# A two-layer "macaron" block with an S4D layer: the second feed-forward's weights and norm parameters are loaded from ACT's DMA queue at set points, and the last scans' temporaries move to another buffer

## The chip, the cores and the metric

The kernel runs on one core of one Trainium2 chip. The core has five engines with a queue each: PE (matrix products), DVE (vector work), ACT (scalar functions and copies), POOL (elementwise work) and SP (here it only issues DMAs). An engine takes its instructions strictly in the order of its queue; engines wait for each other through semaphores. The metric is the device time of one execution in microseconds. Three runs of the kernel before gave 1841.8, 1843.71 and 1846.46; the median is 1843.71.

## The reference

The input x is 8 sequences of 2048 positions with 256 channels.

```python
x = x + 0.5 * ffn(layernorm(x), w1, b1, w2, b2)
x = x + s4d(layernorm(x), log_A_real, A_imag, C_re, C_im, log_dt, D, ln_w, ln_b)
x = x + 0.5 * ffn(layernorm(x), w1, b1, w2, b2)

def ffn(x, w1, b1, w2, b2):
    h = relu(x @ w1 + b1)          # 256 -> 1024
    return h @ w2 + b2             # 1024 -> 256

def s4d(x, ...):                   # a state space model, one filter per channel
    K = s4d_kernel(...)            # 256 channels x 2048 positions, 64 modes each
    y = irfft(rfft(x, 2L) * rfft(K, 2L))[:, :L]     # causal convolution
    r = x + (y + x * D)
    return layernorm(r) * ln_w + ln_b
```

Both feed-forwards use the same weights. The norm's parameters ln_w and ln_b belong to the middle layer; the kernel applies them when it reads that layer's result, at the beginning of the second feed-forward's work on a group.

## The kernel before, in words

**Three stages.** `sublayer(..., "a", ...)` is the first feed-forward, then comes the SSM (the calls of `states` and `outputs`), then `sublayer(..., "b")`. A feed-forward takes the tokens in 64 groups of 256. For each group `pre_a` or `pre_b` normalises and transposes the tokens, `up` multiplies by w1 (bank `ph`), ACT and DVE make the two-part hidden values (buffer `hx`), `down` multiplies by w2 (bank `po`), and `post_a` or `post_b` adds the result. The groups are staggered: `lead` steps of preparation run before the first product.

**The SSM.** The convolution is done in 16 chunks of 128 positions. The 256 channels form 32 batches `bt` of 8 channels (4 pairs), and the batches are put into 12 groups `gr`, listed in `PLAN` with a state buffer (`xsA`, `xsB` or `xsE`) and a part of it. Group 8 is batches 22 to 25, group 9 is batches 26 and 27, group 10 is 28 and 29, group 11 is 30 and 31; group 7 is 20 and 21.
- `states(gr)`: for each batch PE projects the chunks onto the states (bank `pv`, line 972, with the loaded matrices `pt`), ACT copies the result to the state buffer (`keep`, line 955). Then a `scan` runs over the chunks, 14 steps of four instructions each (lines 1008 to 1011): two products with the decay factors into temporaries, and two additions to the next chunk's states. Most pairs are scanned by DVE, some by POOL (`POOL_PAIRS`).
- `outputs(gr)`: for each batch SP loads the matrices `tz` (line 1024) and `ot` (line 1038), ACT copies the channels to `uc` (line 1031), PE sums the part within the chunk (line 1043, `uc` with `tz`) and the part from the states (line 1052, the state buffer with `ot`) in two banks `py`, and ACT writes both back to `u` (line 1058, "the evacuation").

`states` runs ahead of `outputs` by three groups (`AHEAD = 3`): program order is outputs 6, states 9, outputs 7, states 10, outputs 8, states 11, outputs 9, 10, 11.

**Buffers.** Tiles that share a tag share a ring of buffers (`BUFS`): a new tile takes the buffer of the tile that was allocated that many allocations earlier, and its first writer waits for the last reader of the old one. The tag `hx` has 4 buffers: the hidden values of the feed-forwards and the copies `uc` of the SSM. The tags `e` and `te` have one buffer each: the two temporaries of DVE's scan steps, and after the last scan the norm's parameters `lnw_sb` and `lnb_sb`. The large buffers `wA` and `wB` hold the weights of the first feed-forward, then the states A and B, then the weights of the second (`wb1` in `wA`, `wb2` in `wB`), so `wb1` can be written when the last group in A (group 8) has been read, and `wb2` when the last in B (group 10) has.

**Order.** A scheduler orders the instructions of each engine by their readiness; `tc.issue_after` puts an instruction behind another one, and `tc.manual_schedule` keeps the engines that it names in program order. `sublayer` uses the latter for ACT and DVE in its lead if it has a list `first` (the first feed-forward has) or if `MB` is set.

**The reload.** After the last group the kernel writes the DMAs that bring back the split weights from DRAM: eight of 256 KB for w1 and four of 512 KB for w2 on SP's queue (lines 1133 and 1137), and ln_w and ln_b, spread over the partitions, on POOL's queue (line 1143). The second feed-forward's first group needs `lnb_sb` on POOL (line 1152), `lnw_sb` on DVE (`y`), `wb1` in `up` and `wb2` in `down`.

Of the kernel before, what the change touches and what calls it, by code (L numbers as in the profile page):

```python
# [10 lines left out]
F32 = mybir.dt.float32  # L11
F32R = mybir.dt.float32r
# [7 lines left out]
P = 128  # L20
# [23 lines left out]
def macaron_s4d_kernel(  # L44
# [17 lines left out]
    nc = tc.nc  # L62
    V = nc.vector
    A_ = nc.scalar
    G_ = nc.gpsimd

    B, L, H = x.shape
    N = c_re.shape[1]
    W = w1.shape[1]
    NJ = L // P  # L70
# [3 lines left out]
    NDC = H // P  # L74
    NFC = W // P
# [6 lines left out]
    PINW = 1  # L82
    NZ = 1
    PINF = 0
    MB = 0
    PINT = 1
    XY = 4
    NU = NFC // 2
# [16 lines left out]
    wpool = ctx.enter_context(tc.tile_pool(name="wpool", bufs=1))  # L105
# [4 lines left out]
    def bank(tag, name):  # L110
        return ps.tile([P, 512], F32, name=name, tag=tag, bufs=BANKS[tag])

    def slot(tag, shape, name, dtype=F32):
        tag = {"sw": "xn"}.get(tag, tag)
        return work.tile(shape, dtype, name=name, tag=tag, bufs=BUFS[tag])
# [23 lines left out]
    w1_dram = dram.tile([2, P, NDC, W], F32, name="w1_dram")  # L139
    w2_dram = dram.tile([2, P, NFC, H], F32, name="w2_dram")  # L140
# [667 lines left out]
    def sublayer(w1t, w2t, pre, post, lead, tag, first=(), background=(), due=()):  # L808
# [32 lines left out]
        ordered = ExitStack()  # L841
        if first or MB:
            ordered.enter_context(
# [78 lines left out]
    PLAN = [E8, ("A", 0, 8), ("A", 8, 16), B16, E8, A16, B16, E8, A16, ("B", 0, 8), ("B", 8, 16), E8]  # L922
# [2 lines left out]
    assert sum(sizes) == NPAIR  # L925
    starts = [sum(sizes[:i]) for i in range(len(sizes))]
    SPAN = {"A": 16, "B": 16, "E": 8}
    TAGS = ("e", "te")
    POOL_PAIRS = [8, 0, 0, 4, 4, 4, 4, 4, 4, 2, 2, 0]
    LASTX = 11  # L930
    OTS = ("xh", "xh", "pl", "xn"), ("xh", "x", "pl", "x")
    TZS = ("xl", "xl", "pl"), ("xl", "x", "pl")
    BH = 4
    BL = 9
    xbuf = {}
    steps = {}

    BEHIND = [BH] * (len(PLAN) - 1) + [BL]

    def states_of(gr):  # L940
        key, at, end = PLAN[gr]
        if key not in xbuf:
            t = wpool.tile([P, 2, SPAN[key], NJ * B], F32, name=f"xs{key}", tag=f"w{key}")
            G_.memset(t[:, :, :, 0:B], 0.0)
            xbuf[key] = t
        return xbuf[key][:, :, at:end]

    def batches(gr):
        for p0 in range(0, sizes[gr], PB):
            yield p0, (starts[gr] + p0) // PB  # L950
# [6 lines left out]
    def states(gr):  # L957
        xs = states_of(gr)
        for p0, bt in batches(gr):
            pts = []  # L960
            for c in range(2):
                pt = slot("x", [P, PB, P], f"pt{bt}_{c}")
                nc.sync.dma_start(out=pt, in_=pt_dram[bt].rearrange("k (c l m) -> k c l m", c=2, m=P)[:, c])
                pts.append(pt)
            pv = [
                bank(tag, f"pv{bt}_{ri}").rearrange("p (l m) -> p l m", l=PB)
                for ri, tag in enumerate(("oo", "tb")[bt % 2])
            ]
            for l in range(PB):
                for ri in range(2):  # L970
                    for c in range(2):
                        nc.tensor.matmul(
                            pv[ri][c * N : (c + 1) * N, l, :], pts[c][:, l, ri * N : (ri + 1) * N],
                            u[:, :, BCH * bt + 2 * l + c, :],
                            start=True, stop=True, skip_group_check=True,
                        )
            keep(xs, [v[:, :, 0:CB] for v in pv], slice(p0, p0 + PB), slice(B, NJ * B))
        on_dve = sizes[gr] - POOL_PAIRS[gr]
        if on_dve:
            for _ in scan(gr, V, 0, on_dve, 1, NJ - 1, TAGS):  # L980
                pass
        if POOL_PAIRS[gr]:
            for _ in scan(gr, G_, on_dve, sizes[gr], 1, NJ - 1, ("g", "gt")):
                pass
# [4 lines left out]
    def scan(gr, E, p0, p1, j0, j1, tags):  # L989

        n = p1 - p0
        shape = [P, 2, n, B]
        xv = states_of(gr)[:, :, p0:p1].rearrange("p r g (j b) -> p r g j b", b=B)
        gs = slice(starts[gr] + p0, starts[gr] + p1)
        wr_b = wr_c[:, gs].unsqueeze(1).unsqueeze(3).to_broadcast(shape)
        wi_b = wi_c[:, :, gs].unsqueeze(3).to_broadcast(shape)
        for j in range(j0, j1):
            t1, t2 = (
                slot(tag, [P, 2, 8 if tag in ("g", "gt") else 16, B], f"{tag}_{gr}_{j}")[:, :, 0:n]
                for tag in tags  # L1000
            )
            with ExitStack() as behind:
                if E is V and prev(gr) in steps:

                    before = steps[prev(gr)]
                    at = min(BEHIND[gr] + j - j0, len(before) - 1)
                    behind.enter_context(tc.issue_after(before[at].ins))
                E.tensor_mul(t1, xv[:, :, :, j, :], wr_b)  # L1008
                E.tensor_mul(t2, xv[:, ::-1, :, j, :], wi_b)  # L1009
                E.tensor_add(xv[:, :, :, j + 1, :], xv[:, :, :, j + 1, :], t1)  # L1010
                ins = E.tensor_add(xv[:, :, :, j + 1, :], xv[:, :, :, j + 1, :], t2)  # L1011
            if E is V:
                steps.setdefault(gr, []).append(ins)
            yield

    def outputs(gr):
        xs = states_of(gr)
        for p0, bt in batches(gr):
            py, tzs, ucs, ots = [], [], [], []
            for c in range(2):  # L1020
                tz = slot(TZS[gr >= LASTX][(2 * bt + c) % 3], [P, PB, P], f"tz{bt}_{c}")

                row = kpad[BCH * bt + c, 1:]
                nc.sync.dma_start(
                    out=tz,
                    in_=bass.AP(row.tensor, row.offset, [[1, P], [2 * KROW, PB], [1, P]]),
                )
                tzs.append(tz)

                uc = slot("hx", [P, PB, P], f"uc{bt}_{c}")  # L1030
                A_.copy(
                    uc.rearrange("p l (q m) -> p l q m", q=NQ),
                    u[:, :, BCH * bt + c : BCH * (bt + 1) : 2, :].rearrange("p q l m -> p l q m"),
                )
                ucs.append(uc)
            for ri in range(2):
                ot = slot(OTS[gr >= LASTX][(2 * bt + ri) % 4], [P, PB, P], f"ot{bt}_{ri}")
                nc.sync.dma_start(out=ot, in_=o_dram[bt][:, ri * PB * P : (ri + 1) * PB * P])
                ots.append(ot)
            for c in range(2):  # L1040
                py.append(bank("h", f"py{bt}_{c}").rearrange("p (l m) -> p l m", l=PB))
                for l in range(PB):
                    nc.tensor.matmul(
                        py[c][:, l, :], ucs[c][:, l, :], tzs[c][:, l, :],
                        start=(l == 0), stop=False, skip_group_check=True,
                    )

            for l in range(PB):
                for ri in range(2):
                    for c in range(2):  # L1050
                        cs = slice(c * N, (c + 1) * N)
                        nc.tensor.matmul(
                            py[c][:, l, :], xs[cs, ri, p0 + l, :], ots[ri][cs, l, :],
                            start=False, stop=(l == PB - 1 and ri == 1), skip_group_check=True,
                        )
            for c in range(2):

                A_.copy(
                    uo[:, :, bt, :, c::2], py[c].rearrange("p l (q m) -> p q m l", q=NQ)
                )  # L1060

    def some(j0, j1):

# [53 lines left out]
        {"half": NG // 2, "tables": NG * 3 // 4},  # L1117
    )

    for gr in (1, 2, 3):  # L1120
        states(gr)
    for gr in range(len(sizes)):
        outputs(gr)
        if gr and gr + AHEAD < len(sizes):
            states(gr + AHEAD)


    wb1 = wpool.tile([P, 2, NDC, W], F32R, name="wb1", tag="wA")
    wb2 = wpool.tile([P, 2, NFC, H], F32R, name="wb2", tag="wB")
    for f in range(0, W, W // 4):  # L1130
        fs = slice(f, f + W // 4)
        for i in range(2):
            nc.sync.dma_start(out=wb1[:, i, :, fs].bitcast(F32), in_=w1_dram[i][:, :, fs])
    for f in range(0, NFC, 4):
        fs = slice(f, f + 4)
        for i in range(2):
            nc.sync.dma_start(out=wb2[:, i, fs].bitcast(F32), in_=w2_dram[i][:, fs])


    lnw_sb = slot("e", [P, H], "lnw_sb")  # L1140
    lnb_sb = slot("te", [P, H], "lnb_sb")
    for dst, src in ((lnw_sb, ln_w), (lnb_sb, ln_b)):
        nc.gpsimd.dma_start(out=dst, in_=src.partition_broadcast(P))

    def pre_b(g):
        by_dma = g >= DMA_B
# [70 lines left out]
```

## Time and profile before

| what | value |
|---|---|
| three runs | 1841.8, 1843.71, 1846.46 us; median 1843.71 |
| the profiled execution | 1849.43 us; span of its instructions 1847.7 us |
| first feed-forward, to the last down-projection of the chain | 864.7 us |
| SSM, to the last evacuation | 1087.2 us |
| second feed-forward, from its first up-projection | 1097.4 us |
| busy over the span | PE 95%, DVE 86%, ACT 66%, POOL 39% |
| granted TensorE clock, mean | 0.978 |

In rows of the timeline the columns are the start (us from the span's first instruction), the duration of the merged row, the engine, the line, the operation with the tiles that it writes and reads, and the number of merged instructions; what stands in brackets is the idle time before it and what ended it. A row of an `L1043` or `L1052` matmul counts two records for each matmul of the program, so 16 `uc` records and 32 `ot` records are one batch. "SPq" is a DMA issued by SP's queue.

### The profile page before, as it was taken

The numbers are of one execution on the slowest core, as the hardware profiler recorded it, in microseconds if no ns is written. First come the engines' busy times: TensorE is split into PE (matmuls) and PEld (weight loads), VectorE is DVE, ScalarE is ACT, GpSimd is POOL, SyncE is SP. The second block draws the span as 40 slices with busy tenths as digits, with TensorE's granted clock in tenths as the row PEclk, the third lists the DMA queues.
The fourth block names the chain that finished last, engine by engine and source line by source line (L and its number), as shares of the span: only waits on it lengthen the run. The fifth ranks groups of instructions, "written<-read, shape, count | busy, mean of one in ns | idle before, by whom it ended". The sixth has DMA issues, their size and how long they took to land.

```text
span 1847.7 us, 43034 instructions
## 1 busy us (share of the span) xinstructions
PE 1757.2 (95%) x15147; PEld 1721.2 (93%) x15147; DVE 1593.6 (86%) x5027; ACT 1212.3 (66%) x2931; POOL 717.0 (39%) x963
## 2 busy tenths in 40 slices
PE   7999799998899999999999879999999999999998
PEld 7999789898888999998888879999999999999998
DVE  5899997998899977775999958989899999999995
ACT  6776556766676776765555436777777777776675
POOL 1016761888478413211588612222222222222220
PEclk9999899999999999999999979999999999999999
DMA  5112233887787943334788833333333333333331
GB/s 186 41 50 58 59 101 90 229 240 236 213 242 228 265 115 102 98 97 127 241 244 250 261 115 87 92 92 92 93 92 92 92 92 92 92 92 91 91 92 51
DMA packets 299451, 245.44 MB, mean 133 GB/s; under 512 B 169954, under 2 KB 242402, under 8 KB 298722
## 3 DMA queue, kind: packets, MB, share of 16 engines
q1 hardware_dynamic: 297456, 241.75, 44.8%
q8 instruction: 119, 1.95, 0.4%
q0 software_dynamic: 800, 0.67, 0.3%
q14 instruction: 98, 0.80, 0.1%
q10 hardware_dynamic: 978, 0.26, 0.1%
HBM read 91.89 MB, written 111.15 MB: 110 GB/s over the span
## 4 chain that ended last, share of the span: by engine, by line
PE 51%; DVE 9%; issue 3%; DMA 2%; POOL 2%; ACT 1%; SPq 0%; POOLq 0%; DVEq 0%; ACTq 0%
PE ph_b L789 19%; PE po_b L799 19%; PE po_a L799 6%; PE ph_a L789 6%; DVE e L1008 2%; DVE te L1009 2%; DVE xsA L1011 1%; DVE xsA L1010 1%; DVE xsB L1010 1%; DVE xsB L1011 1%; DMA wb<-w_dram 1%; DVE xsE L1011 1%; DMA pt_b<-xp 0%; DVE xsE L1010 0%; POOL xsB L1011 0%
## 5 line engine op out<-in xcount | busy, mean ns | idle before, releaser
L799 PE MATMUL po_a<-wa,hx_a 128*128 128x256 f32 x3072 | 462.1, 288 | 11.1 <-DVE hx_a L859 10.4
L789 PE MATMUL ph_a<-xh_a,wa 128*128 128x256 f32 x2048 | 461.6, 289 | 5.7 <-ACT xh_a L736 3.0
L789 PE MATMUL ph_b<-xh_b,wb 128*128 128x256 f32 x2048 | 443.4, 284 | 1.1 <-ACT xh_b L736 0.7
L799 PE MATMUL po_b<-wb,hx_b 128*128 128x256 f32 x3072 | 443.2, 284 | 0.0
L799 PEld LDWEIGHTS po_a<-wa,hx_a 128*128 128x128 f32 x3072 | 410.0, 195 | 17.6 <-DVE hx_a L859 16.2
L799 PEld LDWEIGHTS po_b<-wb,hx_b 128*128 128x128 f32 x3072 | 400.0, 192 | 0.9
L789 PEld LDWEIGHTS ph_a<-xh_a,wa 128*128 128x128 f32 x2048 | 362.8, 197 | 8.0 <-ACT xh_a L736 3.6
L857 ACT ACTIVATE ph_a<-ph_a,b_sb 128x256 f32<-128x256 f32 x512 | 228.8, 449 | 200.5 <-PE ph_a L789 190.0
L789 PEld LDWEIGHTS ph_b<-xh_b,wb 128*128 128x128 f32 x2048 | 352.9, 193 | 2.1 <-ACT xh_b L736 1.2
L857 ACT ACTIVATE ph_b<-ph_b,b_sb 128x256 f32<-128x256 f32 x512 | 229.8, 449 | 168.3 <-PE ph_b L789 162.3
L789 PE MATMUL ph_a<-xl_a,wa 128*128 128x256 f32 x1024 | 294.7, 290 | 20.9 <-DVE xl_a L770 11.3
L1152 POOL TENSOR_TENSOR xb<-xb,lnb_sb 128x512 f32<-128x512 f32 x64 | 92.4, 1446 | 514.3 <-DMA xb<-x_dram 232.4
L789 PE MATMUL ph_b<-xl_b,wb 128*128 128x256 f32 x1024 | 287.2, 285 | 0.7 <-DVE xl_b L770 0.2
L859 DVE TENSOR_TENSOR hx_a<-ph_a,hx_a 128x256 fp32r<-128x256 f32 x512 | 207.5, 412 | 77.8 <-ACT hx_a L858 76.1
L859 DVE TENSOR_TENSOR hx_b<-ph_b,hx_b 128x256 fp32r<-128x256 f32 x512 | 205.0, 410 | 33.2 <-ACT hx_b L858 31.3
L789 PEld LDWEIGHTS ph_a<-xl_a,wa 128*128 128x128 f32 x1024 | 201.6, 197 | 23.2 <-DVE xl_a L770 12.3
L720 POOL TENSOR_TENSOR xa<-xa,hb 128x512 f32<-128x512 f32 x64 | 84.3, 1317 | 354.9 <-DVE xn_a L694 243.1
L789 PEld LDWEIGHTS ph_b<-xl_b,wb 128*128 128x128 f32 x1024 | 197.5, 193 | 1.9 <-DVE xl_b L770 1.4
L858 ACT CAST hx_a<-ph_a 128x256 fp32r<-128x256 f32 x512 | 188.4, 374 | 13.2 <-PE po_a L799 1.6
L858 ACT CAST hx_b<-ph_b 128x256 fp32r<-128x256 f32 x512 | 187.7, 374 | 11.3
L720 POOL TENSOR_TENSOR xb<-xb,hb 128x512 f32<-128x512 f32 x64 | 87.9, 1373 | 52.4 <-DVE t_r L681 26.3
L118 DVE SCALAR_TENSOR_TENSOR y<-u,mv_r,lnw_sb 128x256 f32<-128x256 f32 x128 | 82.8, 688 | 4.8 <-PE pt_b L727 0.9
(257 smaller groups left out, 2824.9 us busy)
## 6 DMA issues: line engine op xcount, KB each, us to landing
xa<-in_L_attn_x_dram SPq DMA_DIRECT2D x64, 256.0 KB, 2.8
x_dram<-xa SPq DMA_DIRECT2D x64, 256.0 KB, 2.3
o<-u SPq DMA_DIRECT2D x32, 512.0 KB, 4.0
pv<-planes SPq DMA_DIRECT2D x32, 512.0 KB, 3.6
pt<-u SPq DMA_DIRECT2D x32, 512.0 KB, 3.4
ot<-o SPq DMA_DIRECT2D x64, 256.0 KB, 3.7
tz<-kpad SPq DMA_DIRECT2D x64, 256.0 KB, 4.2
xb<-x_dram SPq DMA_DIRECT2D x64, 256.0 KB, 2.7
```

Of the source, the lines that this page charges most:

```text
L118: return V.scalar_tensor_tensor(out=o, in0=a, scalar=s, in1=b, op0=op0, op1=op1)
L720: G_.tensor_add(xt, xt, hb2.unsqueeze(1).to_broadcast([P, NTB, H]))
L789: nc.tensor.matmul(ph, wt[wp][:, dc, fs], xp[:, dc, :], start=(n == 0), stop=(n == 3 * NDC - 1))
L799: nc.tensor.matmul(po[:, i, :], hp[:, tsl], wt[wp][:, fc, :], start=(fc == 0 and i == 0 and n == 0), stop=(fc == NFC - 1 and n == 2), skip ...
L857: A_.activation(ph, ph, AF.Relu, bias=b1_sb[:, fc : fc + 1])
L858: last[A_] = A_.copy(hh, ph)
L859: last[V] = V.tensor_sub(hl, ph, hh.bitcast(F32))
L1008: E.tensor_mul(t1, xv[:, :, :, j, :], wr_b)
L1009: E.tensor_mul(t2, xv[:, ::-1, :, j, :], wi_b)
L1010: E.tensor_add(xv[:, :, :, j + 1, :], xv[:, :, :, j + 1, :], t1)
L1011: ins = E.tensor_add(xv[:, :, :, j + 1, :], xv[:, :, :, j + 1, :], t2)
L1152: G_.tensor_add(xt, xt, lnb_sb.unsqueeze(1).to_broadcast([P, NTB, H]))
```

## The change

The temporaries of DVE's scans from group 9 on (`LASTE = 9`) no longer live in `e` and `te`: both halves of one `hx` tile are used. This leaves `e` and `te` free after group 8, and `lnw_sb` and `lnb_sb` are allocated there. A generator, `late_loads`, issues the loads from ACT's queue in three parts: ln_w and ln_b, then w1 in two DMAs of 1 MB, then w2 in two of 1 MB. Each part is put behind the last evacuation of the first batch of a group: groups 9, 10 and 11. The DMAs on SP's and POOL's queues are gone. `MB = 1` keeps ACT and DVE in program order in the lead of the second feed-forward.

```diff
-    MB = 0
+    MB = 1
...
-    TAGS = ("e", "te")
     POOL_PAIRS = [8, 0, 0, 4, 4, 4, 4, 4, 4, 2, 2, 0]
     LASTX = 11
+    LASTE = 9
...
+    evacs = {}
...
-            for _ in scan(gr, V, 0, on_dve, 1, NJ - 1, TAGS):
+            for _ in scan(gr, V, 0, on_dve, 1, NJ - 1, ("hx",) if gr >= LASTE else ("e", "te")):
...
+            if tags == ("hx",):
+                both = slot("hx", [P, 2, 2, 16, B], f"hx_{gr}_{j}")
+                t1, t2 = (both[:, i, :, 0:n] for i in range(2))
+            else:
+                t1, t2 = (
+                    slot(tag, [P, 2, 8 if tag in ("g", "gt") else 16, B], f"{tag}_{gr}_{j}")[:, :, 0:n]
+                    for tag in tags
+                )
...
-                A_.copy(
+                done = A_.copy(
                     uo[:, :, bt, :, c::2], py[c].rearrange("p l (q m) -> p q m l", q=NQ)
                 )
+            evacs.setdefault(gr, []).append(done)
...
+    def late_loads():
+        for dst, src in ((lnw_sb, ln_w), (lnb_sb, ln_b)):
+            nc.scalar.dma_start(out=dst, in_=src.partition_broadcast(P))
+        yield
+        for i in range(2):
+            nc.scalar.dma_start(out=wb1[:, i].bitcast(F32), in_=w1_dram[i])
+        yield
+        for i in range(2):
+            nc.scalar.dma_start(out=wb2[:, i].bitcast(F32), in_=w2_dram[i])
+        yield
+
+    LOADS = {LASTE: 1, LASTE + 1: 1, len(PLAN) - 1: 1}
     for gr in (1, 2, 3):
         states(gr)
     for gr in range(len(sizes)):
         outputs(gr)
         if gr and gr + AHEAD < len(sizes):
             states(gr + AHEAD)
-    wb1 = wpool.tile([P, 2, NDC, W], F32R, name="wb1", tag="wA")
-    wb2 = wpool.tile([P, 2, NFC, H], F32R, name="wb2", tag="wB")
-    for f in range(0, W, W // 4):
-        fs = slice(f, f + W // 4)
-        for i in range(2):
-            nc.sync.dma_start(out=wb1[:, i, :, fs].bitcast(F32), in_=w1_dram[i][:, :, fs])
-    for f in range(0, NFC, 4):
-        fs = slice(f, f + 4)
-        for i in range(2):
-            nc.sync.dma_start(out=wb2[:, i, fs].bitcast(F32), in_=w2_dram[i][:, fs])
-    lnw_sb = slot("e", [P, H], "lnw_sb")
-    lnb_sb = slot("te", [P, H], "lnb_sb")
-    for dst, src in ((lnw_sb, ln_w), (lnb_sb, ln_b)):
-        nc.gpsimd.dma_start(out=dst, in_=src.partition_broadcast(P))
+        if gr == LASTE - 1:
+            lnw_sb = slot("e", [P, H], "lnw_sb")
+            lnb_sb = slot("te", [P, H], "lnb_sb")
+            wb1 = wpool.tile([P, 2, NDC, W], F32R, name="wb1", tag="wA")
+            loads = late_loads()
+        if gr == LASTE + 1:
+            wb2 = wpool.tile([P, 2, NFC, H], F32R, name="wb2", tag="wB")
+        if gr in LOADS:
+            with tc.issue_after(evacs[gr][0].ins):
+                next(loads)
```

More of the change, by code (lines that the diff above doesn't have):

```diff
@@ L997, in scan @@
         for j in range(j0, j1):
[L998 to L1001, printed above, removed]
+            if tags == ("hx",):
[6 more added lines that the diff above has]
+                )
             with ExitStack() as behind:
```

## The prediction

> **What bounds the kernel now.** I read the busy shares, then the chain of waits, then the timeline of each engine from 1005 us to 1100 us, the seam the change touches. The kernel has three stages: the first feed-forward to 864.7 us, the SSM to 1087.15, the second feed-forward from 1097.37. In the second PE is full (499.76 of 500 us from 1300 to 1800) and the order of the first is not touched, so only the seam can move. In the SSM the chain runs along DVE's scans:
>
> ```profile
> 1026.83 0.31 DVE L1008 TENSOR_TENSOR e<-xsB,wr_c 128x96 f32<-128x96 f32 x1
> 1041.62 0.24 DVE L1008 TENSOR_TENSOR e<-xsB,wr_c 128x96 f32<-128x96 f32 x1
> 1055.61 0.28 DVE L1008 TENSOR_TENSOR e<-xsE,wr_c 128x128 f32<-128x128 f32 x1
> 1070.42 0.29 DVE L1011 TENSOR_TENSOR xsE<-xsE,te 128x128 f32<-128x128 f32 x1
> ```
>
> These are the first instructions of scans 9, 10 and 11 and the last of scan 11: back to back, 14 steps each, 1.056, 1.00 and 1.08 us a step. PE works on outputs beside them:
>
> ```profile
> 1024.90 2.05 PE L1043 MATMUL py<-tz,uc 128*128 128x128 f32 x16
> 1042.25 3.71 PE L972 MATMUL pv<-u,pt 128*64 128x128 f32 x64
> 1050.95 2.05 PE L1052 MATMUL py<-ot,xsB 64*128 64x128 f32 x16
> 1057.03 2.05 PE L1043 MATMUL py<-tz,uc 128*128 128x128 f32 x8 [4.03 <-DMA tz<-kpad]
> 1059.00 3.78 PE L1052 MATMUL py<-ot,xsB 64*128 64x128 f32 x16
> 1081.92 2.05 PE L1043 MATMUL py<-tz,uc 128*128 128x128 f32 x16
> 1083.90 2.06 PE L1052 MATMUL py<-ot,xsE 64*128 64x128 f32 x32
> ```
>
> The four batches 22 to 25 (group 8) stand between the first two rows: 4.34 us a batch, while scan 9 runs. So outputs of group g run during scan g+1, and when scan 11 ends (1070.71) little is left: PE is done at 1085.96. It would have been done sooner but for the 4.03 us wait; after it TensorE runs at half clock:
>
> ```profile
> 1050.00:1055.00 5.00, 3.00 (x24) 2.69 (x24) 4.66 (x22) 2.34 (x4) 0.76 (x4) 0.98 1.09 348
> 1055.00:1060.00 5.00, 2.98 (x12) 2.78 (x13) 4.69 (x21) 0.62 (x1) 0.00 (x0) 0.50 0.80 246
> 1070.00:1075.00 5.00, 5.00 (x30) 4.78 (x30) 0.68 (x3) 1.12 (x2) 1.18 (x2) 0.50 0.64 146
> 1075.00:1080.00 5.00, 5.00 (x58) 4.64 (x57) 0.00 (x0) 2.38 (x4) 2.49 (x2) 0.97 0.61 171
> ```
>
> Columns: PE, PEld, DVE, ACT, POOL busy, then granted clock, DMA share and GB/s. The wait comes from SP's queue, where 2 MB of w1 went just ahead of that `tz`:
>
> ```profile
> 1043.05 2.61 SPq L1133 DMA_DIRECT2D wb<-w_dram  x4
> 1046.84 2.77 SPq L1133 DMA_DIRECT2D wb<-w_dram  x4
> 1049.71 0.55 SPq L1024 DMA_DIRECT2D tz<-kpad  x1
> 1078.66 1.75 SPq L1137 DMA_DIRECT2D wb<-w_dram  x4
> ```
>
> Then a front of 10.2 us from the last evacuation to the first up-projection:
>
> ```profile
> 1086.04 1.11 ACT L1058 COPY u<-py 128x512 f32<-128x512 f32 x2 [2.84 <-PE py L1052]
> 1095.47 1.23 PE L727 MATMUL pt_b<-ident,xn_b 128*128 128x128 f32 x4 [9.52 <-DVE xn_b L694]
> 1097.37 1.23 PE L789 MATMUL ph_b<-xh_b,wb 128*128 128x256 f32 x4 [0.68 <-ACT xh_b L736]
> ```
>
> The reloads themselves are not on the path: the last w2 transfer, issued by 1080.4, landed by 1089.97, and its first reader starts at 1102.65. Nor are the norm's parameters: their POOL additions end at 1078.6 while their DVE readers start at 1088.
>
> **The change, part by part.**
>
> *Buffers, the part that decides.* From group 9 on each scan step takes one of the four `hx` buffers for both temporaries; the copies `uc` of every output batch, two each, rotate through the same four. Rotation follows program order: uc of group 6, scan 9, uc of group 7, scan 10, uc of group 8, scan 11, uc of groups 9, 10, 11. In the changed program as built the waits say just that: uc20_0 waits for step 11 of scan 9, uc20_1, uc21_0 and uc21_1 for steps 12 to 14; uc22_0 for step 11 of scan 10; uc26_0 for step 11 of scan 11; in return, scan 10 waits for the `uc` matmuls of batches 20 and 21, scan 11's first step for those of batch 24 (steps 2, 7 and 9 for 24 and 25). Overlap becomes alternation. PE's order moves too: the projections `pv` of groups 10 and 11 (7.4 us) stand ahead of batch 20, their loads ahead of `tz21_1` on SP. Up to `pv27` (1012.4 us) all engines' orders are unchanged.
>
> *Walk to scan 11.* PE ends pv31 near 1023 (7.4 us of work, and loads that take turns in the `x` buffers) and idles until uc20_0: step 11 of scan 9 ends at 1026.83 + 11 x 1.056 = 1038.45, the copy takes 0.62, PE starts at 1039.1. Sixteen idle microseconds put the clock at half, as the 4.03 did. Prices of matmuls: 16 `uc` records 2.0 us at full clock, 4.0 at half (8 took 1.97 from 1057.03 to 1059.00); 32 `ot` records 2.0 when the two halves alternate, but one half alone costs 2.05 for 16 at full and 3.71 at half (rows 1050.95 and 1059.00), and batches 20, 22 and 26 have such stretches. Batch 20: 2.0 + 2.8 + 2.0 + 3.8 = 10.6, to 1049.7; batch 21: `uc` 4.0, then 2.0 with the clock back, to 1055.5. Scan 10 begins on time, since its first step needs only four `uc` matmuls (1041.2 against 1041.62), and loses about 1 us at steps 10 and 12. ACT is in order: uc22_0 stands behind the evacuation of batch 21, so 1057.4. PE: batch 22 with its serial stretches 5.8, batch 23 4.0, first half of batch 24's `uc` 1.0: scan 11 starts at 1068.3, not 1055.61: **+12.7**. If the clock returns within batch 20, batch 21 is out by 1052 and uc22_0 waits for scan 10 alone: 1064.7, **+9.1**. At half clock throughout: 1059.8 + 21.5 = 1081.3, **+25.7**.
>
> *From the end S of scan 11 to the last evacuation.* Before: 1087.15 - 1070.71 = 16.4. After: six batches, 26 to 31, are still to do, where two were. uc26_0 is there at S - 3 x 1.08 + 0.65 = S - 2.6, PE has idled some 5.5 us (half clock again); batch 26 takes 10.6 to S + 8.0, batch 27 6.0 to S + 14.0, four batches at 4.34 to S + 31.4, evacuation 1.2: S + 32.6, **+16.2**. Clock back 4 us sooner: +12.4. Full clock from the start: 5.5 + 5 x 4.05 + 1.2 - 2.6 = S + 24.4, +8.0. Half clock all through (8.0 a batch): about +35.
>
> *Loads on ACT's queue.* Six issues at 0.38 to 0.70 us (the six ACT-queue rows of the first stage), in evacuation gaps of 1.3 us and more: nothing, as `uc` copies run a batch ahead of PE. The second w2 issue waits for the first w1 half; ACT's evacuation of batch 31 stands behind it. w1 is issued after batch 28, some 8.7 us earlier, and the reloads before took 4.2 to 10.0 us to land: 0 to +2, taken +0.5. w1 and w2 have about 20 and 10 us until their readers; w2's margin is the thin one. SP loses 12 issues and POOL two; the 4.03 us wait behind them goes, but lay beside scan 11, and its benefit is inside the tail's count.
>
> The Trainium skill, page "DMA: Bandwidth & Descriptors", section "Rules for kernel authors", speaks against this part: spreading transfers over issuing engines saves issue time only, all share the same 16 DMA engines. The row that bears on it is the DMA share of 1.09 while w1 and `tz` ran together. By the rule w1 would hold up `tz31` by up to those 4.03 us again; without the rule it is 0.
>
> *Program order in the lead of the second feed-forward.* The first group's chain no longer shares DVE with statistics of groups 1 and 2 (the 1.39 us of st_r at 1091.09, 0.35 of mv_r), but y now follows the reciprocals, and the sqrt of group 1 precedes xh on ACT: -1.8 to 0, taken **-1.0**.
>
> **Sum.** Late release 12.7 + 16.2 + 0.5 - 1.0 = +28.4; release within the first batch 9.1 + 12.4 + 0.5 - 1.0 = +21. In the trace the half clock lasted 18 us after 1057.03, where serial `ot` stretches ran, and some 5 us after 868.57 with `pv` matmuls; the new stretches mix both, so I take the middle, +25. The profiled run took 1849.4 (span 1847.7 + 1.7), 5.7 above the median of 1843.7; it would become 1874, the median **1869**. Floor: 9.1 + 8.0 - 1.8 = +15.3, 1859.
>
> The skill's "TensorE: Matmul & The Clock Gate", Part 1, has the clock return after about 3.4 us of sustained work. The 18 us of half clock from 1057 disagree with it. By the rule each restart costs 1.7 us, the first one hidden behind scan 10, and the sum would be about +17, 1861.
>
> **Rivals.** (a) The clock stays low: serial stretches keep it at half through batches 22 to 26. For it: 18 us at 0.50 above. Against: full-array `uc` stretches of 4 us follow, and 1072.86 to 1075.97 brought the clock back. Price +35 to +45: 1879 to 1889. (b) Weights late: if w2's halves, serialized behind w1 and ACT's evacuations, land after the first down-projection, PE waits there; 10.0 us was the longest landing, so +3 to +8 more, 1872 to 1877. (c) Not slower: the shared rotation costs nothing, scans 10 and 11 stay at 1041.62 and 1055.61, groups 9 and 10 are out during scan 11, SP no longer holds `tz27_1`. Then PE ends two batches after 1070.71: 8.1 + 1.2 = 1080.0, -7.1, and -1.0 at the front: 1836. It decides if scan 11 starts before 1060. Against it stand the waits in the built program. (d) The reload is hidden anyway and nothing moves: true of the loads, not of the buffers.
>
> **Numbers.** Likeliest 0.78 (1859 to 1878), (a) 0.12, (b) 0.05, (c) 0.03, (d) 0.02. Range 1857 to 1884. A difference of 0.3% (5.5 us) is what the measurement can tell from none. Slower 0.95, same 0.02, faster 0.03.
>
> **What would show it.** PE idle from about 1023 to 1039 and again around 1077, each followed by a granted clock of 0.5; `uc` copies of ACT released by DVE scan steps; scan 11's start at 1064 to 1070 and end near 1080 to 1085; six output batches behind it; last evacuation near 1112; front of some 9 us. Wrong if scan 11 starts at 1056, if the front shrinks by more than 3, or if PE waits for `wb`.

## The result, and the profile after

| | before | after |
|---|---|---|
| median of five runs each | 1844.91 us (1841.8 to 1848.44) | 1879.24 us (1876.04 to 1880.59) |
| ratio | 1 | 1.0181, 95% interval 1.0164 to 1.0197 |
| profiled execution, its span | 1849.43, 1847.7 us | 1880.59, 1878.8 us |
| first instruction of scan 9 to the end of scan 11 | 43.88 us | 57.92 us |
| end of scan 11 to the last evacuation | 16.44 us | 34.56 us |
| last evacuation to the first up-projection | 10.22 us | 9.45 us |
| the three together, "the seam" | 70.54 us | 101.93 us |

The change makes the kernel slower: 34.3 us by the medians, 31.1 by the two profiled spans. The seam, taken from the first instruction of scan 9 so that the drift of a few microseconds ahead of it drops out, grew by 31.4 (14.0 + 18.1 - 0.8) and so holds all that the two profiles differ by. The 3 us between spans and medians are not explained: the profiled execution before lay 4.5 us above its median, the one after 1.35. Line numbers of the changed kernel are five higher from the scan's lines on.

The timeline of DVE after the change, with the first instructions of scans 9 and 10, the first one of scan 10 that had to wait, then the first and the last instruction of scan 11:

```profile
1025.59 0.31 DVE L1013 TENSOR_TENSOR hx<-xsB,wr_c 128x96 f32<-128x96 f32 x1
1040.48 0.24 DVE L1013 TENSOR_TENSOR hx<-xsB,wr_c 128x96 f32<-128x96 f32 x1
1050.76 0.26 DVE L1013 TENSOR_TENSOR hx<-xsB,wr_c 128x96 f32<-128x96 f32 x1 [0.89 <-PE py L1048]
1068.41 0.29 DVE L1013 TENSOR_TENSOR hx<-xsE,wr_c 128x128 f32<-128x128 f32 x1 [12.84 <-ACT u L1063]
1083.22 0.29 DVE L1016 TENSOR_TENSOR xsE<-xsE,hx 128x128 f32<-128x128 f32 x1
```

Scans 9 and 10 still stand back to back, but scan 11 has 12.84 us of idle DVE ahead of it. (The profile names ACT's evacuation of batch 23, which ends at 1068.36, as its releaser. By the waits of the built program, as the prediction lists them, it waits for `uc` products of batch 24, the first of which end at 1068.30 by PE's timeline; the two lie too close together for the profile to tell them apart.) PE's timeline shows the other half of the alternation:

```profile
1038.02 2.08 PE L1048 MATMUL py<-tz,uc 128*128 128x128 f32 x8 [14.88 <-ACT uc L1036]
1040.03 2.93 PE L1057 MATMUL py<-ot,xsE 64*128 64x128 f32 x12
1048.60 3.78 PE L1048 MATMUL py<-tz,uc 128*128 128x128 f32 x16
1057.27 1.16 PE L1048 MATMUL py<-tz,uc 128*128 128x128 f32 x8 [2.47 <-ACT uc L1036]
1063.18 2.05 PE L1048 MATMUL py<-tz,uc 128*128 128x128 f32 x16
1081.05 2.08 PE L1048 MATMUL py<-tz,uc 128*128 128x128 f32 x8 [5.21 <-ACT uc L1036]
1091.62 3.27 PE L1048 MATMUL py<-tz,uc 128*128 128x128 f32 x16
1108.41 2.06 PE L1057 MATMUL py<-ot,xsE 64*128 64x128 f32 x32 [1.14 <-DMA ot<-o]
1112.85 2.02 PE L1048 MATMUL py<-tz,uc 128*128 128x128 f32 x16 [2.39 <-DMA tz<-kpad]
```

The first, fourth and sixth rows are the starts of batches 20, 22 and 26, each released by a copy `uc`. The copy itself is released by DVE's scan, as ACT's timeline says; the rows after it are the loads on ACT's queue and the last evacuation:

```profile
1037.35 0.62 ACT L1036 COPY uc<-u 128x512 f32<-128x512 f32 x1 [18.71 <-DVE xsB L1016]
1080.38 0.62 ACT L1036 COPY uc<-u 128x512 f32<-128x512 f32 x1 [3.34 <-DVE xsE L1016]
1101.46 0.82 ACTq L1133 DMA_DIRECT2D wb<-w_dram  x2
1110.63 0.81 ACTq L1136 DMA_DIRECT2D wb<-w_dram  x2
1116.95 1.12 ACT L1063 COPY u<-py 128x512 f32<-128x512 f32 x2 [5.31 <-PE py L1057]
```

So DVE's scan waits for the output batches, the output batches wait for the scan, and 14.88 and 5.21 us of PE's time and 12.84 of DVE's are spent waiting. After each long wait the granted clock is low (windows of the changed kernel; columns as in the prediction: PE, PEld, DVE, ACT, POOL busy, granted clock, DMA share, GB/s):

```profile
1045.00:1050.00 5.00, 5.00 (x26) 4.78 (x27) 4.47 (x18) 1.72 (x4) 4.22 (x19) 0.50 0.32 84
1055.00:1060.00 5.00, 2.73 (x22) 2.60 (x22) 0.54 (x3) 4.39 (x9) 0.00 (x0) 1.00 0.46 138
1085.00:1090.00 5.00, 5.00 (x24) 4.55 (x24) 0.00 (x0) 0.62 (x1) 0.00 (x0) 0.50 0.23 61
1100.00:1105.00 5.00, 5.00 (x70) 4.76 (x70) 0.00 (x0) 2.41 (x5) 0.00 (x0) 1.00 0.97 286
```

In the last, full-clock window PE gets through 70 records, in the half-clock ones through 24 to 26; the ratio is more than two because the half-clock windows also hold stretches of `ot` matmuls on one half. After the short wait of 2.47 us (second row) the clock is at 1. The front is the last part:

```profile
1125.52 1.23 PE L727 MATMUL pt_b<-ident,xn_b 128*128 128x128 f32 x4 [8.66 <-DVE xn_b L694]
1127.52 1.23 PE L789 MATMUL ph_b<-xh_b,wb 128*128 128x256 f32 x4 [0.78 <-ACT xh_b L736]
```

No wait for `wb` follows: the weights were there in time.

### The profile page after: what moved, and what is told of

Its sections match the earlier page's. It is cut to its first block, busy times and chain, and to the rows that moved or that the text cites. A ratio compares the mean times of both kernels' runs of the same rounds, so it can differ in the third digit from the quotient of the medians.

```text
span 1878.8 us, 43020 instructions
## 1 busy us (share of the span) xinstructions
PE 1760.8 (94%) x15147; PEld 1725.3 (92%) x15147; DVE 1601.2 (85%) x5027; ACT 1211.5 (64%) x2931; POOL 718.9 (38%) x961
## 4 chain that ended last, share of the span: by engine, by line
PE 56%; DVE 7%; DMA 3%; issue 1%; ACT 1%; DVEq 0%; SPq 0%; ACTq 0%
PE ph_b L789 19%; PE po_b L799 19%; PE po_a L799 6%; PE ph_a L789 6%; PE py L1057 2%; PE py L1048 2%; DMA tz<-kpad 2%; DVE e L1013 1%; PE pv L973 1%; DVE te L1014 1%; DVE xsA L1016 1%; DVE xsA L1015 1%; DVE xsB L1016 0%; DVE xsB L1015 0%; PE pe L1102 0%
## 5 line engine op out<-in xcount | busy, mean ns | idle before, releaser
L799 PEld LDWEIGHTS po_a<-wa,hx_a 128*128 128x128 f32 x3072 | 408.4, 194 | 16.2 <-DVE hx_a L859 15.0
L789 PEld LDWEIGHTS ph_a<-xl_a,wa 128*128 128x128 f32 x1024 | 200.7, 196 | 23.8 <-DVE xl_a L770 12.7
L858 ACT CAST hx_a<-ph_a 128x256 fp32r<-128x256 f32 x512 | 188.1, 374 | 13.3 <-PE po_a L799 1.6
L1048 PE MATMUL py<-tz,uc 128*128 128x128 f32 x512 | 77.3, 302 | 30.6 <-ACT uc L1036 22.6
```

The costliest lines, as they stand in the source:

```text
L789: nc.tensor.matmul(ph, wt[wp][:, dc, fs], xp[:, dc, :], start=(n == 0), stop=(n == 3 * NDC - 1))
L799: nc.tensor.matmul(po[:, i, :], hp[:, tsl], wt[wp][:, fc, :], start=(fc == 0 and i == 0 and n == 0), stop=(fc == NFC - 1 and n == 2), skip ...
L858: last[A_] = A_.copy(hh, ph)
L1048: nc.tensor.matmul(py[c][:, l, :], ucs[c][:, l, :], tzs[c][:, l, :], start=(l == 0), stop=False, skip_group_check=True,)
```

## The experiments

The kernels ran on three chips, each beside runs of the kernel before on the same chip: own_temps to kept_warm on one, own_sp_loads to late_w1 on the second, the last three on the third. Medians of different chips are best compared by the ratio. The seam is read from each kernel's profiled execution as above; T is the end of scan 11 to the last evacuation, F the front.

| run | scan 9 to end of 11 | T | F | seam | median us | ratio to before, 95% interval |
|---|---|---|---|---|---|---|
| before | 43.88 | 16.44 | 10.22 | 70.54 | 1845.17, 1844.85, 1842.59 on the three chips | |
| after | 57.92 | 34.56 | 9.45 | 101.93 | 1879.24 | 1.0164 to 1.0197 |
| own_temps | 46.02 | 9.71 | 8.44 | 64.17 | 1834.42 | 0.9917 to 0.9961 |
| ring_sp_loads | 58.07 | 30.43 | 10.36 | 98.86 | 1875.32 | 1.0129 to 1.0180 |
| ring_from_11 | 43.73 | 36.29 | 9.48 | 89.50 | 1861.52 | 1.0065 to 1.0107 |
| kept_warm | 58.09 | 31.01 | 9.41 | 98.51 | 1872.95 | 1.0113 to 1.0166 |
| own_sp_loads | 47.07 | 13.37 | 10.27 | 70.71 | 1846.36 | 0.9990 to 1.0014 |
| own_warm | 45.78 | 7.27 | 8.49 | 61.54 | 1838.20 | 0.9939 to 0.9973 |
| late_w1 | 62.03 | 31.05 | 8.42 | 101.50 | 1870.77 | 1.0116 to 1.0161 |
| own_again | 46.03 | 9.54 | 8.75 | 64.32 | 1835.34 | 0.9952 to 0.9976 |
| own_warm_again | 46.00 | 7.28 | 9.52 | 62.80 | 1835.84 | 0.9943 to 0.9975 |
| own_warm_front | 46.15 | 8.33 | 8.41 | 62.89 | 1832.11 | 0.9930 to 0.9957 |

**own_temps: the ring taken away.**

```diff
-            for _ in scan(..., ("hx",) if gr >= LASTE else ("e", "te")):
+            for _ in scan(..., ("c", "ct") if gr >= LASTE else ("e", "te")):
```

"c" and "ct" are two new tags with one buffer each; the room comes from halving POOL's temporaries "g" and "gt", whose second half is not used. All else is the changed kernel.

> The changed kernel, but the temporaries of scans 9 to 11 have two small buffers of their own (room for them comes from halving POOL's temporaries, which use half); loads on ACT's queue and program order in the lead stay. Theory (the ring of four hx buffers is the loss): uc copies no longer wait for scans, scan 11 starts some 28.8 us after scan 9 as before, two batches are left when it ends, w1 no longer delays tz27: last evacuation 4 to 9 us earlier than before, time 1835 to 1842. Rival (late loads on ACT's queue and their collision with tz and ot are the loss): 1865 or more.

1834.42 us, faster than both kernels. Scan 11 follows scan 10 directly again and only batches 30 and 31 are left behind it, as PE's timeline of own_temps shows:

```profile
1063.02 2.05 PE L1048 MATMUL py<-tz,uc 128*128 128x128 f32 x16
1070.78 3.79 PE L1057 MATMUL py<-ot,xsE 64*128 64x128 f32 x32 [5.71 <-DVE xsE L1016]
1074.50 2.75 PE L1048 MATMUL py<-tz,uc 128*128 128x128 f32 x16
1077.17 2.06 PE L1057 MATMUL py<-ot,xsE 64*128 64x128 f32 x32
```

PE now waits 5.71 us for the scan, where before the scan had ended (1070.71) 9 us ahead of PE's first product that needs it (1079.93). The shared ring is therefore the whole loss, and the rest of the change is a gain.

PE still waits for the second `tz` of batch 27, though, as the same timeline shows, and no weights are on their way here (w1 is first issued at 1059.25):

```profile
1050.45 1.13 PE L1048 MATMUL py<-tz,uc 128*128 128x128 f32 x8 [2.52 <-DMA tz<-kpad]
1051.51 3.29 PE L1057 MATMUL py<-ot,xsB 64*128 64x128 f32 x32
```

**ring_sp_loads: the ring alone with the old loads.** The changed kernel, with the reload on SP's and POOL's queues after the last group as before (the removed block put back, `late_loads` no longer called).

> The changed kernel with its temporaries in the hx ring and program order in the lead, but the twelve weight DMAs on SP's queue and the norm's parameters on POOL's, written after the last group as before. Theory: the ring keeps its price of 12.7 to 14 at scan 11 and some 16 in the tail; the 3.5 us for which PE waited for tz and ot beside w1 may go or stay: 1872 to 1881. Rival (the loads on ACT's queue are the loss): 1842 to 1848.

1875.32 us, seam 98.86: the loads on ACT's queue are not the cause of the loss. Beside the changed kernel's 101.93 they do cost 3.1 us in the ring: T is 30.43 with the old loads, 34.56 with the new ones, while the front is 0.9 longer with the old ones.

**ring_from_11: the ring for the last scan only.**

```diff
-            for _ in scan(..., ("hx",) if gr >= LASTE else ("e", "te")):
+            for _ in scan(..., ("hx",) if gr >= 11 else ("e", "te")):
```

> The changed kernel with only scan 11 in the hx ring; scans 9 and 10 keep their old buffers. Theory: two terms come apart. Scan 11 starts some 28.8 us after scan 9 as before (term +14 gone), uc26 to uc27 still wait for its steps 11 to 14, so six batches are left behind it (term +18 stays): 1859 to 1867. Rival (the price hangs on the delay of the scans alone): 1842 to 1848. Rival (it is all in the last ring turn): 1876 to 1880.

1861.52 us. The two large terms come apart: the way to the end of scan 11 is the kernel before's (43.73 beside 43.88) and all 19 us of the longer seam lie behind it. PE's timeline of ring_from_11:

```profile
1059.09 2.07 PE L1048 MATMUL py<-tz,uc 128*128 128x128 f32 x8 [21.21 <-ACT uc L1036]
1091.04 2.50 PE L1048 MATMUL py<-tz,uc 128*128 128x128 f32 x16 [3.67 <-DMA tz<-kpad]
```

PE is done with group 8 already and sits 21.21 us until step 11 of scan 11 frees a buffer for `uc26_0`; then the six batches follow as in the changed kernel.

**kept_warm: the ring without the second half-clock stretch.**

```diff
+        if gr == LASTE:
+            idle = bank("h", "idle")
+            for i in range(20):
+                nc.tensor.matmul(idle[:, 0:P], ident, u[:, :, i, :], start=True, stop=True, ...)
```

> The changed kernel with 20 extra matmuls, about 5 us, whose result nobody reads, between batch 25 and batch 26, where PE idles before the half clock. Theory (half clock costs some 6 us of the tail: batch 26 took 10.6 us and batch 27 5.2 instead of some 5.8 and 4.0): batch 28 starts 5 to 6 us earlier, 1872 to 1875. Rival (PE is paced by the uc copies or by its loads there): 1877 to 1881.

1872.95 us. The extra products fill the wait ahead of batch 26 and the clock stays at 1. Batches 26 and 27 take 9.8 us (1078.62 to 1088.39) where the changed kernel needs 15.8 (1081.05 to 1096.81). PE's timeline of kept_warm, the extra products and a later row:

```profile
1074.05 4.73 PE L1026 MATMUL idle<-u,ident 128*128 128x128 f32 x40
1104.73 3.50 PE L1055 MATMUL py<-tz,uc 128*128 128x128 f32 x16 [2.42 <-DMA tz<-kpad]
```

Of the 6 us, 3.6 show in T: the extra products hold batch 26 up by 0.7 us, the waits for `tz` are still there, and the last of them (2.42 us) drops the clock again, so that 16 records take 3.50 us. The median fell by 6.3 us against the changed kernel's, the seam by 3.4; the profile does not show the rest.

**own_sp_loads: own temporaries with the old loads.** own_temps with the reload as in the kernel before; PE's and SP's order is then the kernel before's.

> The last scans' temporaries in buffers of their own, the weights and the norm's parameters loaded as in the kernel before (SP's and POOL's queues, after the last group), the lead of the second feed-forward in program order. PE's and SP's order is the kernel before's. Theory (what own_temps won over the kernel before came from the loads' move, because tz27_1 no longer stands behind 2 MB of w1 on SP's queue, PE does not wait 4 us there and does not fall to half clock): the wait of about 4.0 us and some 18 us of half clock are back, PE is again the last at the end of scan 11, and only the front's gain of about 1 us is left: 1843 to 1845 beside 1845 of the kernel before. Rival (the gain came from the program order in the lead or from e and te being free early): 1834 to 1837. Rival (the loads' place is worth nothing, and own_temps gained from PE's changed order): also 1834 to 1837, but then without a wait for tz27_1.

1846.36 us, the kernel before's time. The wait and the half clock are back on PE's timeline:

```profile
1048.98 2.05 PE L1048 MATMUL py<-tz,uc 128*128 128x128 f32 x8 [3.29 <-DMA tz<-kpad]
1050.96 3.78 PE L1057 MATMUL py<-ot,xsB 64*128 64x128 f32 x16
```

So what own_temps wins comes with the loads' move, not with the buffers or the lead's program order. Of the 6.5 us between the two seams, 3.7 are T, 1.8 the front and 1.1 the way to the end of scan 11. The wait for `tz` itself is only 0.8 us shorter in own_temps (2.52 beside 3.29). What differs more is what follows it: from the end of that wait to the end of batch 29, own_sp_loads needs 21.0 us (to 1070.02) and own_temps 12.6 (to 1063.02). In own_temps the scheduler has put batches 27 and 28 in an order where the halves of `ot` alternate, and the granted clock, 0.50 from 1052.5 to 1055, is back at 1.00 from 1057; in own_sp_loads it is 0.50 from 1050 to 1066. How much of this is the order and how much the shorter wait was not separated. The front did not get shorter here (10.27); why, the last section says.

**late_w1: the changed kernel with w1 issued later.**

```diff
-    LOADS = {LASTE: 1, LASTE + 1: 1, len(PLAN) - 1: 1}
+    LOADS = {LASTE: 1, len(PLAN) - 1: 2}
```

> The changed kernel, with the two w1 loads issued together with the two of w2, behind the first evacuation of group 11 instead of group 10. Theory (in the changed kernel the 2 MB of w1 held up ot31 and tz31, 1.14 and 2.39 us, and nothing needs w1 so early): 3.0 to 3.5 us less than the changed kernel, about 1876, and no wait for ot31 or tz31. Rival (those waits come from the issue order on SP's queue, not from w1's transfer): unchanged, 1879. Rival (w1 and w2 together land too late for the first up- or down-projection): 2 to 5 us more, with PE waiting for wb.

T falls by 3.5 us, with no wait for `ot31` or `tz31` left: those waits were w1's transfer. The front is 8.42. Yet the seam is 101.50, since on the way to scan 11 the clock fell to half for batch 22, as PE's timeline of late_w1 shows (in the changed kernel the second of these rows took 2.05 and the third 2.05):

```profile
1052.34 1.16 PE L1048 MATMUL py<-tz,uc 128*128 128x128 f32 x8 [2.48 <-ACT uc L1036]
1057.84 3.78 PE L1057 MATMUL py<-ot,xsA 64*128 64x128 f32 x18
1061.55 3.52 PE L1048 MATMUL py<-tz,uc 128*128 128x128 f32 x16
```

The median of 1870.77 is 8.5 below the changed kernel's, more than the 3.0 to 3.5 expected; its five runs spread over 10.4 us, and what makes up the rest stays open.

**own_warm, and once more beside own_again.** own_temps, with 22 such unread products at the start of `outputs(11)`.

> own_temps, and 22 extra products of u with the identity, which nobody reads, on PE ahead of the first product of group 11, in the 5.7 us that PE waits for scan 11 there. Theory (after that wait PE runs at half clock, which costs 1.7 us in the ot products of batch 30, 0.7 us in the uc products of batch 31, and nothing after): 2.4 us less than own_temps, about 1832; the granted clock stays at 1 from 1060 to 1080 us. Rival (the loads of w2 and the evacuations set the end there): the same as own_temps, 1834. Rival (the extra products run past the end of scan 11): up to 2 us more.

> own_temps once more, for a comparison on one chip with the next two. Theory (the seam from scan 9 to the first up-projection takes 64.2 us in it and 70.5 in the kernel before, and nothing else differs): 6 to 10 us less than the kernel before, 1835 to 1839. Rival (the 1834 of the first time was a favourable chip): 1840 or more.

> own_warm once more (22 unread products ahead of group 11), beside own_temps on one chip. Theory (its seam is 61.5 us beside 64.2): 2 to 3 us less than own_again. Rival (the seam's gain is given back later, or the difference is that of single executions): the same as own_again within 1 us.

In the traces the mechanism holds: T is 7.27 and 7.28 instead of 9.71 and 9.54. In the time it can't be seen: own_warm's 1838.20 missed the 1832 expected, and on one chip it is 1835.84 beside 1835.34. In the second pair the front was 0.8 longer with the extra products, so the seams differ by 1.5 only.

**own_warm_front: the front filled as well.** own_warm, and 30 more unread products after the last output batch.

> own_warm, and 30 more unread products of u with the identity after the last output batch, ahead of the second feed-forward's first transposition, where PE waits 7.7 us for xn_b and is at half clock afterwards. Theory (the first group's up-projections then run at full clock: the rows from the first ph_b to the first po_b take about 3 us instead of 5.8): 2 to 3 us less than own_warm_again. Rival (the first down-projection waits for ACT's and DVE's hidden values or for w2's landing, so the time goes into a wait): the same as own_warm_again. Rival (the extra products delay the first transposition): up to 2 us more.

The theory fell. The first transposition does run at full clock, but the clock is lost right behind it (PE's timeline, then two windows of own_warm_front):

```profile
1073.34 6.96 PE L1167 MATMUL idle<-u,ident 128*128 128x128 f32 x60
1081.06 0.87 PE L727 MATMUL pt_b<-ident,xn_b 128*128 128x128 f32 x4 [0.75 <-DVE xn_b L694]
1083.05 0.74 PE L789 MATMUL ph_b<-xh_b,wb 128*128 128x256 f32 x4 [1.12 <-ACT xh_b L736]
1084.45 0.58 PE L789 MATMUL ph_b<-xl_b,wb 128*128 128x256 f32 x1 [0.66 <-DVE xl_b L738]
```

```profile
1080.00:1085.00 5.00, 2.47 (x13) 1.65 (x13) 4.78 (x20) 1.06 (x3) 1.26 (x1) 0.87 0.00 0
1085.00:1090.00 5.00, 5.00 (x26) 5.00 (x25) 3.88 (x15) 3.28 (x8) 0.00 (x0) 0.50 0.02 3
```

Three pauses of 0.75, 1.12 and 0.66 us around a few products are enough, and from the first `ph_b` to the first `po_b` it takes 5.83 us (own_warm_again 5.49). The median of 1832.11 is the lowest of all, but the profile shows no cause for the difference to own_warm_again: T is 1.05 us longer, the front 1.11 shorter, the seams are equal within 0.1, and the two intervals overlap. The version to keep is own_temps: 11 and 7 us below the kernel before on two chips.

## Why the prediction held, point by point

The median of 1879.24 lies in the stated range (1857 to 1884), but above the interval of the likeliest case (1859 to 1878) and just inside the price of rival (a), 1879 to 1889. The traces show the likeliest case's mechanism, not that of (a).

**Walk to scan 11: right.** The branch "late release" came true step by step. Batch 20 was put at 10.6 us and took 10.58 (1038.02 to 1048.60); batch 22 started at 1057.27, not 1057.4; batches 22 and 23 took 5.9 and 4.0 beside 5.8 and 4.0; scan 11 was put at 1068.3 and began at 1068.41. That the times agree so closely is partly luck: scan 9 had started 1.2 us earlier, and counted from there scan 11 began after 42.8 us, not 41.5. The term is +14.0, not +12.7.

**Tail: right, a little small.** `uc26_0` released PE at S - 2.5 (predicted S - 2.6), batch 26 was done at S + 8.1 (S + 8.0), batch 27 at S + 13.3 (S + 14.0). The four batches behind it took 20.1 us instead of 17.4: 16.3 of work, 3.8 of waits for `tz` and `ot`. Together +18.1 instead of +16.2.

**Loads on ACT's queue: the issues free, the collision mis-sized.** The six issues took 0.36 to 0.41 us each and no wait behind them shows. The part was taken as +0.5 with nothing for the collision, and the collision cost 3.5 us (1.14 + 2.39), which late_w1 took away. The prediction weighed a rule of the Trainium skill here ("DMA: Bandwidth & Descriptors", "Rules for kernel authors": another queue saves issue time, the transfer shares the same engines), by which it would be up to 4.03. The runs agree with the rule, with 3.5, and the sum should have carried it.

**Front: right in sum.** -0.8 beside -1.0, but made up of two things, one of which the prediction did not have (last section).

**The step that was off: the middle.** The prediction formed two sums, +21 and +28.4, and took +25 because the stretches were thought to mix both kinds of matmul. Nothing mixed: all terms went with the late case, and 28.4 with the collision's 3.5 and without the 0.5 is 31.4, the seam's growth. That this fits to the tenth is luck again: the way to scan 11 was put 1.3 us too low and the tail without the collision 1.6 too high (16.2 beside 18.1 - 3.5). The other reading weighed, the Trainium skill's "TensorE: Matmul & The Clock Gate", Part 1 (clock back after some 3.4 us), is off here: from 1038.02 the records take the half-clock time until 1052.31, over 14 us.

**Rivals.** (a) the clock was low for two stretches, but came back in each. (b) no wait for `wb`. (c), the faster case, was wrong for this kernel and near its price once the ring is gone: in own_temps T falls by 6.7 us, from 16.44 to 9.71 (predicted -7.1), the front by 1.8 (predicted -1.0), the way to the end of scan 11 grows by 2.1 (predicted 0), and the time is 1834 or 1835 (predicted 1836). The wait for the second `tz` of batch 27, which (c) had gone, is still 2.52 us there. (d) fell.

## What to carry to other kernels

Before a temporary is moved into a ring that another engine rotates through, write the allocations of that ring down in program order: each entry waits for the readers of the entry so many places back, and a pair of engines that ran side by side then takes turns. Price it by what becomes late (here six output batches behind the last scan instead of two), and price the restart at half clock with it. The order of the program is not the whole of it, though. Step 3 of scan 11 began at 1070.68, before the `uc` products of batch 25 began (1071.45), whose first buffer would have been next in turn. So the ring did not turn strictly one place at a time here, and the waits of the built program have to be read too. A part that loses as a bundle can still hold a gain: the loads' move is worth some 7 to 11 us once the temporaries have buffers of their own.

## What the runs showed of the hardware

**POOL's additions hold DVE up.** In own_sp_loads the front kept its 10.27 us although DVE's program order was the shorter one. DVE's timeline there, then POOL's:

```profile
1084.90 1.18 DVE L118 SCALAR_TENSOR_TENSOR q_fb<-q_fb,s_fb 128x2 f32<-128x2 f32 x1
1086.32 1.44 DVE L694 TENSOR_SCALAR xn_b<-xb,mv_fb,t_fb 128x256 f32<-128x256 f32 x2
```

```profile
1083.59 3.70 POOL L1172 TENSOR_TENSOR xb<-xb,lnb_sb 128x512 f32<-128x512 f32 x3 [29.10 <-DMA xb<-x_dram]
```

The same two DVE rows of late_w1, where no POOL addition runs beside them:

```profile
1119.89 0.16 DVE L118 SCALAR_TENSOR_TENSOR q_fb<-q_fb,s_fb 128x2 f32<-128x2 f32 x1
1120.29 0.73 DVE L694 TENSOR_SCALAR xn_b<-xb,mv_fb,t_fb 128x256 f32<-128x256 f32 x2
```

These two rows are 1.0 and 0.7 us longer beside POOL's additions than in late_w1. Not every DVE row is held: in own_temps an addition runs from 1084.69 to 1085.95, and the BATCH_NORM_AGGREGATE (0.30) and RECIPROCAL (0.17) rows beside it take as long as the same rows of late_w1, which have none beside them. (The Trainium skill, page "SBUF — State Buffer", section "Who interferes with whom", says that the two engines share a pair of ports as an exclusive lock; the rows agree with a lock held for about one 1.27 us addition, but which port a row used is not in the trace.) This goes with the spread of the fronts of the eleven kernels with program order in the lead: 8.4 to 8.5 where no row is held, 8.75 in own_again, where one is held by 0.3, 9.4 to 9.5 in the changed kernel and three others, where one is held by about 1.0, 10.3 and 10.4 with some 2 us of it. Less what the held rows are longer, all of them are 8.3 to 8.5. In the changed kernel the held row is `y` (0.88 in own_temps), as DVE's and POOL's timelines show:

```profile
1120.32 1.91 DVE L118 SCALAR_TENSOR_TENSOR y<-u,mv_r,lnw_sb 128x256 f32<-128x256 f32 x2
1120.69 1.26 POOL L1167 TENSOR_TENSOR xb<-xb,lnb_sb 128x512 f32<-128x512 f32 x1 [2.20 <-issue]
```

An undisturbed front is thus 1.8 us shorter than the 10.22 of the kernel before, and the changed kernel gave 1.0 of that back. Not all of the 1.8 is the program order's: in the kernel before a row was held too (`q_fb` at 1093.84 took 0.71), which leaves some 1.2 us by estimate. No run tried the additions by themselves. The same hold fits the 2.1 us that scans 9 to 11 take longer in own_temps (46.02): the norm's parameters are there early, two additions run during scan 11, and its first two products take 1.38 and 1.36 us instead of 0.28.

**The clock after a pause.** After the same 2.47 or 2.48 us of idle PE ahead of batch 22 the clock stayed at 1 in the changed kernel and fell to 0.5 in late_w1. How soon it comes back differs too: in own_temps, where the halves of `ot` alternate, the rows after 1070.78 are back at 2.06 within 6.4 us; in the changed kernel, with one half at a time, it took over 14 us from 1038.02. That the kind of matmul is the reason is a reading of these stretches; no run tried it.
